# A static schedule for a two-layer mixture-of-experts block: a third group's rows ahead of the last group's, longer gathers in the cost table, constants made at the start

## The chip, the cores and the metric

The kernel runs on one core of a Trainium2 chip. The time is the device time of one launch in microseconds (us): 592.65 us is the median of three runs of the kernel before (590.98 to 595.71). One further execution was recorded by the hardware profiler; it took 534.51 us, and every duration and every point in time below is from that execution, counted from the start of its span.

The engines are named PE (TensorE, matrix products), DVE (VectorE), ACT (ScalarE), POOL (GpSimd) and SP (SyncE, which only issues DMA here). Each runs its own instructions in the order in which they stand in the program, and waits on semaphores for the others.

## The reference

Input are 8 sequences of 256 tokens with 128 features (2048 tokens), float32. Six layers follow each other:

```
x = x + 0.5 * moe(layernorm(x))          # layer 0: 8 experts, top 2 of 8 for every token
x = x + attention(layernorm(x))          # 16 heads of 8, causal
x = x + 0.5 * moe(layernorm(x))          # the same weights again: layer 1
x = x + 0.5 * mix(layernorm(x))          # channel mixing with the token before
x = x + shift(layernorm(x))              # 9 gated shifts (0, +-1, +-4, +-16, +-32), own layernorm
x = x + 0.5 * mix(layernorm(x))

def moe(y):                              # y: rms-normalised rows
    p = top2(softmax(y @ router.T))      # weights of the two experts, summing to 1
    for e in range(8):
        g, u = split(y @ gate_up[e].T)   # 352 hidden features each
        out += p[:, e] * ((silu(g) * u) @ down[e].T)
    return y + clip(alpha) * out

def mix(y):                              # y1: y moved by one token
    r = sigmoid((mu_r*y + (1-mu_r)*y1) @ W_r)
    k = square(relu((mu_k*y + (1-mu_k)*y1) @ W_k))
    return r * (k @ W_v)

def shift(y):
    v = y @ value_W
    out = sum over 9 shifts s of roll(v, -s) * sigmoid(y @ gate_W[s])
    return layernorm(out) * gamma + beta
```

## The kernel before

**Tiling.** The 2048 tokens are 4 groups (`NG`) of 4 x 128 rows (`GT`, `P`). The residual of group g stays on chip as `x[g]` (in the profile x0 to x3 are x_69 to x_72, or plainly x). Dense parts run group by group. In the expert layers each token has two assignments, so 4096 rows are sorted by expert into tiles of 128 rows; with padding these are `TILES` = 39 tiles a layer, every one with one expert.

**An expert layer.** `moe_route` normalises a group, stores its rows to DRAM (`rows0` for the first two groups, `rows1` for all), and finds the top two experts with a product `pl` and DVE's max instructions. `moe_plan` is made twice: once for the first two groups (`whole=False`), which fixes `few` = 9 tiles that these groups fill completely, and once for all groups (`whole=True`), which fixes the other 30. It counts rows per expert, gives every assignment a slot (`end`, `full`, `base`, `until`, `up`, `past`, `slot`), turns the slots into source rows by comparisons (`hit`, `val`, `at`) and small products `pi`, and writes the row lists `take0`, `take1` and the tile's expert. Nearly all of it is DVE work. `moe_experts` then gathers each tile's rows (`xs<-rows,take`, one indirect DMA a tile, issued from POOL), transposes them (`pt`), and `moe_tile` runs the products `pg`, `pu`, the gate `sg`, `hid`, the transposes `ph`, `hT`, the product `po<-dw,hT`, and stores the tile to DRAM by `ys<-ys` from SP. `moe_back` gathers, for each of a group's 4 row blocks and each of the two assignments, the result row by slot (`back<-ys,slot`, 8 indirect DMAs a group, from POOL) and adds it to `x[g]` on DVE.

Slots are ordered so: tiles that groups 0 and 1 fill completely, of which 9 are sure whatever the routing and make the first plan; then one more tile for every expert, which finishes these two groups (tile 24 at the latest); then the rest. So `moe_back` for groups 0 and 1 reads `ys` only up to tile `2*GT*first + E` = 24; groups 2 and 3 read all 39.

**Attention and the last three layers.** `attention` makes two masks, a column of ones `onerow`, and fills the padding of `va` and `mpad` (memsets on POOL); these constants wait for `begun`, an operation of the first layer's weights (`hold["affined"]`). `mix` and `shift` follow per group. In `shift` nine products `pgt` are gated to `p` on DVE; `FOLD` says how many of them POOL adds up (`q`) before PE sums them into one bank with identity products (`po<-ident,q`): (4, 4, 1) means two sums of four and one single, so 3 additions into the bank.

**The order.** `Work` is a list scheduler that runs when the program is built: every operation has an engine, an assumed cost in us, needs, and buffers it takes; the ready operation that can start first goes first, a higher rank (longest path to the end, plus the bias in `BIAS`) wins within 0.3 us. The result is a fixed order on each engine. `BIAS[g]` raises the rank of group g's `moe_back`, `mix` and `shift`; `BIAS[4]` and `BIAS[5]` do so for layer 1's routing and plans. Indirect gathers are entered with 0.98 us on POOL and land 2.7 us (`lag`) later. Where PE would idle in this plan, `keep_warm` puts dummy products `pw<-before,ones_b` in the gap. The recording helper is line 63, which is why all rows name L63.

Of the kernel before, what the change touches and what calls it, by code (L numbers as in the profile page):

```python
# [8 lines left out]
F32 = mybir.dt.float32  # L9
# [10 lines left out]
P = 128  # L20
NG = 4
# [11 lines left out]

BIAS = (25.0, 30.0, 40.0, 55.0, 20.0, 2.0, -6.0)
HC = (0, 128, 224)
ROUND = float(3 * 2**22)
NH = 16
# [7 lines left out]
RMS_EPS = 1e-6  # L47


FOLD = ((4, 4, 1), (4, 4, 1), (4, 4, 1), (4, 2, 1, 1, 1))  # L50


class InOrder:
# [164 lines left out]
def tile_macaron(ctx: ExitStack, tc: tile.TileContext, a: dict, out: bass.AP):  # L218
# [121 lines left out]
    def bank(shape, name):  # L340
        return ps.tile(shape, F32, tag="b", name=name)
# [112 lines left out]
    def moe_layer(n, first):  # L454

        few = 2 * GT * first - 7
        r = {
            "n": n, "first": first, "few": few, "stored": {}, "all_stored": {}, "topped": {},
            "plan": {}, "hold": {},
        }  # L460
        for name, shape, dtype in (
            ("top", [P, NT, 8], F32), ("which", [P, NT, 8], U32), ("w", [P, NT, 2], F32),
            ("ab", [P, 2, NT], F32), ("rs", [P, NT], F32), ("slot", [P, 2 * NT], U32),
            ("take0", [P, few], U32), ("take1", [P, TILES - few], U32), ("expert", [1, TILES], I32),


            ("end", [P, E], F32), ("full", [P, 2, E], F32), ("base", [P, E], F32),
            ("both", [P, E], F32),
        ):
            r[name] = ctile(f"{name}_{n}", shape, dtype)  # L470
        for name, rows in (
            ("rows0", GT * first * P), ("rows1", NT * P), ("ys", TILES * P),
        ):
            r[name] = dram.tile([rows, P], F32, name=f"{name}_{n}", tag=f"{name}_{n}")
        return r
# [126 lines left out]
    def moe_plan(r, whole):  # L602


        few = r["few"]
        nt = NT if whole else GT * r["first"]
        n0, n1 = (few, TILES) if whole else (0, few)
        ns = n1 - n0
# [3 lines left out]
        def small(name, shape, dtype=F32):  # L612

            sizes = dict(zip("abc", shape[1:]))
            wide = 2 * NT * (TILES - 9)
            width = dict(
                oh=2 * NT * E, m=NT * E, slot=NT * E, past=2 * NT * E, sums=P, hit=wide, val=wide,
                le=3 * E, ef=1, eg=1, cb=E, nr=2 * E, at2=2 * E, up=2 * E,
                until=3 * E, whole=E,
            ).get(name, 2 * NT)  # L620
            rows = 1 if shape[0] == 1 else P
            room = wk.tile([rows, width], dtype, tag=name, name=name, bufs=1)
            n = 1
            for m in shape[1:]:
                n *= m
            v[name] = room[0 : shape[0], 0:n]
            if len(sizes) > 1:
                v[name] = v[name].rearrange(
                    f"p ({' '.join(sizes)}) -> p {' '.join(sizes)}", **sizes
                )  # L630
            return v[name]
# [34 lines left out]
        def place():  # L666

            sums = v["sums"]
            pp = bank([P, nt + 1, E], "pp")
            nc.tensor.matmul(  # L670
                pp[:, nt, :], lhsT=sums, rhs=same_e[0 : nt * E], start=True, stop=True
            )
            flat = pp.rearrange("p t e -> p (t e)")[:, 0 : nt * E]
            nc.tensor.matmul(flat, lhsT=before, rhs=v["m"], start=True, stop=False)
            nc.tensor.matmul(
                flat, lhsT=sums, rhs=earlier[0 : nt * E, 0:nt, :].rearrange("p t e -> p (t e)"),
                start=False, stop=True,
            )
            return pp
# [26 lines left out]
        def all_ends():  # L706
            full = r["full"]
            nc.vector.tensor_scalar(full[:, 1, :], full[:, 0, :], float(P), None, ALU.add)
            nc.vector.tensor_tensor(r["both"], r["base"], full[:, 0, :], ALU.add)

            left = small("cb", [P, E])
            nc.vector.tensor_tensor(left, placed.out[:, nt, :], full[:, 0, :], ALU.subtract)
            nc.vector.tensor_scalar(left, left, 63.5, 1.0 / P, ALU.add, ALU.mult)
            nc.vector.tensor_scalar(left, left, ROUND, ROUND, ALU.add, ALU.subtract)
            nr = small("nr", [P, 2, E])
            nc.vector.tensor_scalar(nr[:, 0, :], left, 1.0, None, ALU.min)
            nc.vector.tensor_tensor(nr[:, 1, :], left, nr[:, 0, :], ALU.subtract)

            until = small("until", [P, 3, E])
            nc.vector.tensor_copy(until[:, 0, :], r["end"])  # L720
            for k in range(2):
                nc.vector.tensor_tensor_scan(
                    until[:, k + 1, :], one8, nr[:, k, :], until[:, k, E - 1 : E], ALU.mult, ALU.add
                )


            at2 = small("at2", [P, 2, E])
            nc.vector.tensor_tensor(at2, until[:, 1:3, :], nr, ALU.subtract)
            up = small("up", [P, 2, E])
            nc.vector.scalar_tensor_tensor(  # L730
                up[:, 0, :], at2[:, 0, :], float(P), r["both"], ALU.mult, ALU.subtract
            )
            nc.vector.tensor_tensor(up[:, 1, :], at2[:, 1, :], at2[:, 0, :], ALU.subtract)
            nc.vector.tensor_scalar(up[:, 1, :], up[:, 1, :], -1.0, float(P), ALU.add, ALU.mult)

        def all_slots():
            each, twice = [P, nt, E], [P, nt, 2, E]
            pp, past, slot = placed.out[:, 0:nt, :], small("past", twice), small("slot", each)
            nc.vector.tensor_tensor(
                past, pp.unsqueeze(2).to_broadcast(twice),  # L740
                r["full"].unsqueeze(1).to_broadcast(twice), ALU.is_ge,
            )
            nc.vector.tensor_tensor(past, past, v["up"].unsqueeze(1).to_broadcast(twice), ALU.mult)
            nc.vector.tensor_tensor(slot, pp, r["base"].unsqueeze(1).to_broadcast(each), ALU.add)
            nc.vector.tensor_tensor(past[:, :, 0, :], past[:, :, 0, :], past[:, :, 1, :], ALU.add)
            nc.vector.tensor_tensor(slot, slot, past[:, :, 0, :], ALU.add)

        ended = w.dve(2.4 if whole else 0.9, all_ends if whole else ends, placed, uses=[bp])
        spotted = w.dve(
            1.7 if whole else 0.75, all_slots if whole else slots, ended, uses=[bp]  # L750
        )

        def rows():
# [70 lines left out]
        def which_expert():  # L824


            until = v["until"] if whole else r["end"].unsqueeze(1)
            m = E * (3 if whole else 1)
            le, ef = small("le", [P, m]), small("ef", [P, 1])
            nc.vector.tensor_scalar(  # L830
                le, until.rearrange("p k e -> p (k e)"), float(-n0), tok1[:, 0:1], ALU.add,
                ALU.is_lt,
            )
            nc.vector.tensor_reduce(out=ef, in_=le, axis=AX.X, op=ALU.add)
            if whole:
                eg = small("eg", [P, 1])
                nc.vector.tensor_scalar(eg, ef, -3.5, 1.0 / E, ALU.add, ALU.mult)
                nc.vector.tensor_scalar(eg, eg, ROUND, ROUND, ALU.add, ALU.subtract)
                nc.vector.scalar_tensor_tensor(ef, eg, -float(E), ef, ALU.mult, ALU.add)
# [23 lines left out]
    def moe_experts(r, sizes):  # L863
# [4 lines left out]
        for h in range(2):  # L868
            plan = r["plan"][h]
            rows = r["all_stored" if h else "stored"].values()  # L870
            for n in sizes[h]:
# [14 lines left out]
                got = []  # L886
                for j in range(n):
                    got.append(w.pool(
                        0.98, lambda h=h, k=k0, j=j, f=gather: f(h, k, j), plan["taken"], *rows,
                        **(dict(takes=[xb]) if j == 0 else dict(uses=[xb])), lag=2.7,  # L890
                    ))

# [115 lines left out]
    def moe_back(g, r, stored):  # L1008

        plan, hold = r["plan"][1], r["hold"][g]  # L1010

        until = 2 * GT * r["first"] + E if g < r["first"] else TILES

        def own_rows():
            for t in range(GT):
# [7 lines left out]
        for c in range(2):  # L1023
# [3 lines left out]
            def gather(t, c, box=box):  # L1027
                if t == 0:
# [6 lines left out]

            got = [
                w.pool(
                    0.98, lambda t=t, c=c, f=gather: f(t, c), plan["slots"], *stored[:until],
                    **(dict(takes=[bb]) if t == 0 else dict(uses=[bb])), lag=2.7,
                )  # L1040
                for t in range(GT)
# [15 lines left out]
    BLOCKS = ((0, 0), (1, 0), (1, 1))  # L1057
    LAG = 7

    def attention(begun):  # L1060

# [3 lines left out]
        def constants(mask, step):  # L1067
# [5 lines left out]


        masks = [
            w.pool(1.3, lambda m=m, step=step: constants(m, step), begun)
            for m, step in ((mask_q, -1), (mask_k, 1))
        ]

# [2 lines left out]
            lambda: nc.vector.tensor_reduce(  # L1082
                out=onerow, in_=ident.rearrange("p (j r) -> p j r", r=32)[:, :, DK], axis=AX.X,
                op=ALU.add,
            ), begun,
        )

        va_free = [
            [w.pool(1.4, lambda v=v: nc.gpsimd.memset(v[:, :, :, DK:32], 1.0), begun)] for v in va
        ]  # L1090

        mpad_free = [
            [[w.pool(0.5, lambda m=m: nc.gpsimd.memset(m, 0.0), begun)] for m in row]
            for row in mpad
        ]

# [544 lines left out]
    stored = moe_experts(r0, [[1, 1, 2, *turns(r0["few"] - 4)], turns(TILES - r0["few"])])  # L1641
    for g in range(NG):
        moe_back(g, r0, stored)
    outs = attention(r0["hold"][0]["affined"])
    for g in range(NG):
        changes(g, *outs[2 * g : 2 * g + 2])
        w.back = -BIAS[4] if g < r1["first"] else -BIAS[5]
# [91 lines left out]
```

## Time and profile before

| | us |
|---|---|
| median of three runs (590.98 to 595.71) | 592.65 |
| profiled execution: time | 534.51 |
| its span, first to last instruction | 532.6 |
| PE busy in it | 493.7 (93%) |
| DVE / ACT / POOL busy | 321.5 / 254.2 / 229.7 |
| dummy products pw, 119 of them | 33.6 |
| xs gathers, 78 on POOL: busy, mean | 75.1, 0.962 |
| back gathers, 64 on POOL: busy, mean | 61.4, 0.959 |

The stages, by the timeline: loads, routing and plans of layer 0 to 33 us; its expert tiles from 33 to some 160 us, with attention entered at 122; attention to 302; layer 1's tiles from 300 to 427; mix, shift and mix from 404 to 528; the last store after that. Mean granted TensorE clock is 0.971 of full speed.

A row of the timeline gives start, duration, engine, line, operation, output<-inputs, shapes and count, and in brackets how long the engine stood idle before it and whose event ended the idle time. A busy PE includes the dummy products, which compute nothing that is used; idle time is therefore read as gaps plus `pw` rows.

### The profile page before, as it was taken

The page shows a single profiled execution, that of the slowest core. Times are in us where ns is not written, and L with a number is a line of the kernel's source. Part 1 is how long each engine was busy: PE and PEld are TensorE (multiplying, and loading weights), DVE is VectorE, ACT ScalarE, POOL GpSimd, SP SyncE. Part 2 cuts the span into 40 slices and gives each one's busy share as a digit, 9 for nine tenths or more (in the row PEclk, how much of TensorE's full clock was granted, in tenths as well). Part 3 has the DMA queues.
Part 4 walks back from the last instruction along what each step waited for, and adds up shares of the span by engine and source line. Part 5 has one row for each costly group of instructions (what it writes and reads, how often), then busy time and mean ns, then how long its engine had stood idle before and what let it go on. Part 6 is the DMA issues. An engine that isn't in the chain of part 4 may idle for free.

```text
span 532.6 us, 12554 instructions
## 1 busy us (share of the span) xinstructions
PE 493.7 (93%) x4619; PEld 350.4 (66%) x4619; DVE 321.5 (60%) x1139; ACT 254.2 (48%) x536; POOL 229.7 (43%) x239
## 2 busy tenths in 40 slices
PE   7969989889999999999999999979998996999985
PEld 3537767676776767777777775758775842667564
DVE  7768333455857886777774577333353333878981
ACT  3223455535155446456545641465445572464743
POOL 5150789675005600000002502795373368677641
PEclk9779999999999999999999998999998999899998
DMA  8830222232001100000100110313431011000001
GB/s 282 294 95 26 75 59 59 54 72 51 14 16 46 48 2 3 2 22 3 61 4 11 36 51 18 92 46 72 55 79 31 12 49 45 0 1 1 2 23 57
DMA packets 27035, 26.24 MB, mean 49 GB/s; under 512 B 4064, under 2 KB 24288, under 8 KB 26560
## 3 DMA queue, kind: packets, MB, share of 16 engines
q1 hardware_dynamic: 21232, 15.60, 9.2%
q0 software_dynamic: 4544, 9.32, 8.0%
q8 instruction: 38, 0.62, 0.5%
q10 hardware_dynamic: 1200, 0.53, 0.4%
q14 instruction: 21, 0.17, 0.1%
HBM read 17.18 MB, written 9.31 MB: 50 GB/s over the span
## 4 chain that ended last, share of the span: by engine, by line
PE 58%; POOL 15%; DVE 10%; issue 7%; DMA 6%; ACT 3%; POOLq 0%; SPq 0%; ACTq 0%; DVEq 0%
PE sc L63 15%; PE po L63 11%; PE pg L63 7%; PE pu L63 6%; POOL back L63 6%; PE pt L63 4%; PE ph L63 4%; POOL q L63 2%; PE pr L63 2%; DMA rows<-n 2%; POOL xs L63 2%; DVE stats L63 2%; DMA rest<-in_rest 2%; PE pw L63 2%; PE pk L63 2%
## 5 line engine op out<-in xcount | busy, mean ns | idle before, releaser
L63 POOL DMA_INDIRECT xs<-rows,take x78 | 75.1, 962 | 120.2 <-DVE take L63 41.8
L63 POOL DMA_INDIRECT back<-ys,slot x64 | 61.4, 959 | 59.7 <-DMA ys<-ys 34.3
L63 ACT ACTIVATE ep<-sc 128x512 f32<-128x512 f32 x96 | 52.0, 595 | 55.7 <-PE sc L63 55.7
L63 PEld LDWEIGHTS po<-dw,hT 128*128 128x128 f32 x468 | 62.8, 192 | 21.2 <-ACT hT L63 5.5
L63 PE MATMUL po<-dw,hT 128*128 x468 | 65.9, 279 | 5.3 <-ACT hT L63 3.8
L63 DVE TENSOR_TENSOR hid<-sg,pu 128x352 f32<-128x352 f32 x78 | 40.3, 519 | 48.8 <-PE pu L63 34.6
L63 POOL TENSOR_TENSOR stats<-stats,minus_half 128x4 f32<-128x4 f32 x28 | 28.6, 1023 | 87.7 <-DVE stats L63 87.3
L63 ACT COPY hT<-ph 128x384 f32<-128x384 f32 x78 | 37.1, 477 | 58.1 <-PE ph L63 54.7
L63 PE MATMUL pg<-gu,nT 128*128 x156 | 61.6, 477 | 0.5 <-ACT nT L63 0.5
L63 PE MATMUL pu<-gu,nT 128*128 x156 | 60.5, 470 | 0.0
L63 PEld LDWEIGHTS sc<-kT,qT 32*128 32x128 f32 x768 | 45.8, 186 | 19.2 <-issue 16.4
L63 ACT ACTIVATE sg<-pg 128x352 f32<-128x352 f32 x78 | 36.0, 463 | 41.0 <-PE pg L63 38.3
L63 PE MATMUL sc<-qT,kT 32*128 32x128 f32 x768 | 55.5, 283 | 0.0
L63 PE MATMUL sc<-kT,qT 32*128 32x128 f32 x768 | 54.6, 283 | 0.9 <-DVE mpad L63 0.9
L63 DVE TENSOR_REDUCE mtmp<-sc 128x4 f32<-128x512 f32 x64 | 41.5, 685 | 20.3 <-PE sc L63 20.0
L63 PEld LDWEIGHTS sc<-qT,kT 32*128 32x128 f32 x768 | 46.5, 186 | 2.1 <-issue 2.1
L63 PE MATMUL ph<-ident,hid 128*128 128x128 f32 x234 | 39.1, 279 | 4.4 <-DVE hid L63 4.4
L63 PEld LDWEIGHTS ph<-ident,hid 128*128 128x128 f32 x234 | 29.2, 144 | 17.9 <-DVE hid L63 6.9
L63 PE MATMUL pw<-before,ones_b 128*128 128x512 bf16 x119 | 33.6, 433 | 7.0 <-DVE p L63 4.5
L63 DVE COPY ys<-po 128x128 f32<-128x128 f32 x78 | 21.9, 288 | 21.6 <-PE po L63 17.0
L63 PE MATMUL pgt<-yTg,rest 128*128 128x512 f32 x72 | 33.4, 597 | 0.3 <-ACT yTg L63 0.2
L63 PEld LDWEIGHTS pu<-gu,nT 128*128 128x128 f32 x156 | 26.7, 196 | 7.3 <-issue 0.9
(197 smaller groups left out, 880.9 us busy)
## 6 DMA issues: line engine op xcount, KB each, us to landing
ys<-ys SPq DMA_DIRECT2D x78, 64.0 KB, 1.6
gu<-in_guT SPq DMA_DIRECT2D x2, 1408.0 KB, 8.1
rest<-in_rest SPq DMA_DIRECT2D x1, 1280.0 KB, 8.4
xs<-rows,take POOLq DMA_INDIRECT x78, 2.6
x<-in_x SPq DMA_DIRECT2D x4, 256.0 KB, 4.4
dw<-in_dwT SPq DMA_DIRECT2D x1, 1024.0 KB
rows<-rows SPq DMA_DIRECT2D x2, 512.0 KB
back<-ys,slot POOLq DMA_INDIRECT x64, 2.6
```

The source lines that it names most:

```text
L63: ins = do(*args, **kw)
```

## The change

Five edits:

1. In layer 1, the whole plan gets a third part (`soon` = 3): after the tiles that finish groups 0 and 1 come tiles that group 2's rows fill further, ahead of those that need the last group's. One more product counts the rows of groups 0 to 2, and DVE gets more small instructions and one wider comparison and product (`past` has 3 parts in place of 2). `moe_back` of group 2 then reads `ys` only up to tile `2*GT*3 + E` = 32.
2. Gathers are entered in the schedule with 1.25 us in place of 0.98.
3. Attention's constants no longer wait for `begun`.
4. `BIAS` has new values: the groups' are 10, 28, 18, 0 in place of 25, 30, 40, 55; routing and plan of layer 1's last two groups get 22 in place of 2, those of its first two 19 in place of 20.
5. Group 1's shift is folded as (2, 2, 2, 2, 1) in place of (4, 4, 1).

```diff
-BIAS = (25.0, 30.0, 40.0, 55.0, 20.0, 2.0, -6.0)
+BIAS = (10.0, 28.0, 18.0, 0.0, 19.0, 22.0, -6.0)
-FOLD = ((4, 4, 1), (4, 4, 1), (4, 4, 1), (4, 2, 1, 1, 1))
+FOLD = ((4, 4, 1), (2, 2, 2, 2, 1), (4, 4, 1), (4, 2, 1, 1, 1))
...
+        soon = first + 1 if n == 1 and first + 1 < NG else None
...
-            ("end", [P, E], F32), ("full", [P, 2, E], F32), ("base", [P, E], F32),
+            ("end", [P, E], F32), ("full", [P, 3, E], F32), ("base", [P, E], F32),
...
     def moe_plan(r, whole):
-        few = r["few"]
+        few, soon = r["few"], r["soon"] if whole else None
+        parts = 3 if soon else 2
...
         def place():
+            if soon:
+                rows = slice(0, GT * soon * E)
+                nc.tensor.matmul(
+                    pp[:, nt + 1, :], lhsT=sums[rows, :], rhs=same_e[rows], start=True, stop=True
+                )
...
         def all_ends():
-            nc.vector.tensor_scalar(nr[:, 0, :], left, 1.0, None, ALU.min)
-            nc.vector.tensor_tensor(nr[:, 1, :], left, nr[:, 0, :], ALU.subtract)
+            nc.vector.tensor_scalar(nr[:, 0, :], left[:, 0, :], 1.0, None, ALU.min)
+            if soon:
+                nc.vector.tensor_tensor(nr[:, 2, :], left[:, 0, :], nr[:, 0, :], ALU.subtract)
+                nc.vector.tensor_scalar(nr[:, 1, :], left[:, 1, :], -1.0, 0.0, ALU.add, ALU.max)
+                nc.vector.tensor_tensor(nr[:, 2, :], nr[:, 2, :], nr[:, 1, :], ALU.subtract)
+                nc.vector.scalar_tensor_tensor(
+                    full[:, 2, :], nr[:, 1, :], float(P), full[:, 1, :], ALU.mult, ALU.add
+                )
+            else:
+                nc.vector.tensor_tensor(nr[:, 1, :], left[:, 0, :], nr[:, 0, :], ALU.subtract)
...
-            for k in range(2):
+            for k in range(parts):
                 nc.vector.tensor_tensor_scan(
...
+            if soon:
+                nc.vector.tensor_tensor(up[:, 2, :], up[:, 2, :], nr[:, 1, :], ALU.subtract)
+                nc.vector.tensor_scalar(up[:, 2, :], up[:, 2, :], float(P), None, ALU.mult)
         def all_slots():
-            each, twice = [P, nt, E], [P, nt, 2, E]
+            each, twice = [P, nt, E], [P, nt, parts, E]
...
-            nc.vector.tensor_tensor(past[:, :, 0, :], past[:, :, 0, :], past[:, :, 1, :], ALU.add)
-            nc.vector.tensor_tensor(slot, slot, past[:, :, 0, :], ALU.add)
+            for k in range(parts):
+                nc.vector.tensor_tensor(slot, slot, past[:, :, k, :], ALU.add)
...
-                        0.98, lambda h=h, k=k0, j=j, f=gather: f(h, k, j), plan["taken"], *rows,
+                        1.25, lambda h=h, k=k0, j=j, f=gather: f(h, k, j), plan["taken"], *rows,
...
     def moe_back(g, r, stored):
-        until = 2 * GT * r["first"] + E if g < r["first"] else TILES
+        until = TILES
+        if g < r["first"]:
+            until = 2 * GT * r["first"] + E
+        elif r["soon"] and g < r["soon"]:
+            until = 2 * GT * r["soon"] + E
...
-                    0.98, lambda t=t, c=c, f=gather: f(t, c), plan["slots"], *stored[:until],
+                    1.25, lambda t=t, c=c, f=gather: f(t, c), plan["slots"], *stored[:until],
...
-    def attention(begun):
+    def attention():
-            w.pool(1.3, lambda m=m, step=step: constants(m, step), begun)
+            w.pool(1.3, lambda m=m, step=step: constants(m, step))
...
-            [w.pool(1.4, lambda v=v: nc.gpsimd.memset(v[:, :, :, DK:32], 1.0), begun)] for v in va
+            [w.pool(1.4, lambda v=v: nc.gpsimd.memset(v[:, :, :, DK:32], 1.0))] for v in va
...
-            [[w.pool(0.5, lambda m=m: nc.gpsimd.memset(m, 0.0), begun)] for m in row]
+            [[w.pool(0.5, lambda m=m: nc.gpsimd.memset(m, 0.0))] for m in row]
```

**What it does to the order** (read from the two programs' instruction lists; no time is in them). POOL: the masks and memsets stand ahead of the first gather of layer 0, two of the `mpad` fills and one of `va` between the second and third power instruction of routing. In layer 1, the 16 back gathers of groups 0 and 1 (group 1's first) are followed directly by group 2's eight, and group 3's eight come after group 1's `x += rv`; the last two of them stand behind group 2's `x += rv`. Group 3's first gather waits on seven store semaphores again. PE: before, the mix products of groups 0 and 1 stand among the last layer-1 tiles; in the changed kernel only group 1's do, at the same tile (36 `pg` done), and after the last tile come the mix products of groups 0 and 2, then group 1's shift. Dummies: 24 become 33 at the whole plan of layer 1; after the last tile 3 + 28 + 3 become 3 + 3 + 4, and at the end 3 + 3 + 2 become 3 + 13 + 3. The groups are stored in the order 1, 2, 0, 3 in place of 3, 1, 0, 2.

## The prediction

> **What bounds the kernel now.** I read the page's slices first. PE is the busiest row, at 9 tenths almost everywhere from the tenth slice on, so the end is set by PE's work plus the stretches where PE does nothing useful.
>
> ```profile
> PE   7969989889999999999999999979998996999985
> ...
> PEclk9779999999999999999999998999998999899998
> ```
>
> The 35th slice (440 to 453 us) is the lowest after the start. The windows by stage show it (columns: stretch, its length, busy us and count of PE, PEld, DVE, ACT, POOL, then granted clock, DMA share, GB/s), and the same windows for the dummy products alone show how much of "busy" is empty (PE busy, clock, DMA).
>
> ```profile
> 318.00:328.00 10.00, 9.51 (x59) 5.01 (x57) 9.48 (x43) 0.00 (x0) 0.00 (x0) 1.00 0.01 2
> ...
> 427.00:441.00 14.00, 13.54 (x37) 5.92 (x35) 5.15 (x20) 10.50 (x24) 9.95 (x11) 1.00 0.18 47
> 441.00:455.00 14.00, 8.71 (x35) 3.80 (x35) 6.63 (x24) 2.52 (x7) 11.76 (x12) 0.85 0.16 39
> 455.00:509.00 54.00, 53.64 (x273) 36.80 (x272) 46.78 (x144) 31.10 (x67) 37.68 (x33) 0.98 0.00 1
> ```
>
> ```profile
> 318.00:328.00 10.00, 5.18 (x24) 1.00 0.01 2
> ...
> 441.00:455.00 14.00, 7.40 (x31) 0.85 0.16 39
> ```
>
> So there are two holes: 318 to 328, where DVE is full (9.48 of 10), and 441 to 455, where POOL is (11.76 of 14). The timeline of PE, then of POOL, explains the second:
>
> ```profile
> 435.26 5.31 PE L63 MATMUL pgt<-yTg,rest 128*128 128x512 f32 x12
> 441.59 6.20 PE L63 MATMUL pw<-before,ones_b 128*128 128x512 bf16 x28 [1.02 <-DVE p L63]
> 448.80 1.48 PE L63 MATMUL pt<-ident,y 128*128 128x128 f32 x4 [1.01 <-ACT y L63]
> 453.81 1.44 PE L63 MATMUL pw<-before,ones_b 128*128 128x512 bf16 x3 [3.52 <-DVE p L63]
> 455.04 0.64 PE L63 MATMUL pr<-wrp,yTs 128*128 128x128 f32 x2
> ```
>
> ```profile
> 429.76 1.02 POOL L63 DMA_INDIRECT back<-ys,slot  x1 [0.34 <-issue]
> ...
> 450.79 0.95 POOL L63 DMA_INDIRECT back<-ys,slot  x1 [0.30 <-issue]
> 451.75 2.50 POOL L63 TENSOR_TENSOR q<-p 128x512 f32<-128x512 f32 x2
> ```
>
> The last tile's store leaves at 427.1; 2.7 us later groups 2 and 3 begin 16 gathers, one each 1.25 us (0.94 busy, 0.30 between), and POOL is not free for sums until 451.75. Groups 0 and 1 feed PE until 440.6, then nothing is ready. The first hole ends here; POOL stood idle 23.42 us for the plan:
>
> ```profile
> 328.12 1.02 POOL L63 DMA_INDIRECT xs<-rows,take  x1 [23.42 <-DVE le L63]
> ```
>
> **What the Trainium skill says.** "TensorE: Matmul & The Clock Gate", Part 1, says that an idle window of about 3.4 us halves PE's clock. The trace agrees: behind the hole pairs of `pr` products come every 0.43 us, later in the same run every 0.22. "SBUF — State Buffer", Who interferes with whom, says that a DVE instruction with two SBUF inputs and a GpSimd instruction that reads SBUF exclude each other. The trace agrees in kind: `x<-back,w,x` takes 0.342 us in the median and up to 1.36. "Perfetto Trace Analysis", DMA Instruction — SWDGE, says the reported end of such a DMA is the end of descriptor writing, not of the transfer; a back gather lands 2.5 us after issue in the median.
>
> **The change part by part**, against the profiled execution's 534.5 us.
>
> (1) *Constants early.* Between the gathers of layer 0 (78.0 to 96.9 us) the masks and memsets stretch six intervals to 2.01, 1.70, 1.67, 2.98, 3.78 and 2.59 us; six plain ones are 7.5, one `rs` power in between costs 1.59, so 14.73 - 7.5 - 1.59 = 5.6 us leave POOL's row. PE's own gaps between 56 and 136 us sum to 6.8; those whose cause is POOL or a gather (1.99 and 0.56 via DVE's wait for `rs`, 0.58 via `w`, 1.92 for xs) to 5.1. Value: -1.5, ends 0 and -5. What the early place costs: 0.54 + 0.54 + 1.39 = 2.5 us ahead of the third power, of which 0.94 was idle. I cost it at nothing: rows go out and weights come in by DMA until 33.45, where `pg` starts. Without that cover it would be 1.5.
>
> (2) *Longer whole plan.* Six more small DVE instructions of about 0.17 us, spaced about 0.2: 1.2. Two `past` instructions grow from 256 to 384 elements (0.28 at 128, 0.42 at 256, so about 0.56): 0.3. One more addition: 0.3. Sum 1.8, all on the path, since the first hole is DVE's; queued behind on DVE are the `hid` of three tiles, and behind these PE. The extra count product (0.17) is hidden beside it. Ends +1.2 and +3. `pi` of the first plan stands one score batch (2 us) later on PE; the same hole absorbs it as long as six tiles still fit in front (they took 302 to 317.8). Ends 0 and +2.
>
> (3) *One mix fewer among the tiles.* The mix of one group is pt 0.44, pk 1.72, pr 1.78, pv 0.9 = 4.85 us on PE and moves behind the last tile: the last tile ends earlier and later work grows by as much, net 0. The gap at 402.2 (2.0 us for `y`, whose power stood behind all 16 gathers until 402.37) goes: the power now stands behind 13. Value -2, ends -2.5 and 0. Last tile: 427.0 + 1.8 - 4.85 - 2.0 = 421.9.
>
> (4) *Group 2's gathers early.* Back gathers began at 382.4 (store of tile 24 landed at 381.4); now 384.2. Sixteen of them and one power (1.3 with its gap) end at 405.5. Tile 32's store: the 34th `po` is due around 403 with landing. So group 2's eight run 405.5 to 415.5, land by 418, and its `y` reaches PE near 423.5, while group 0's mix runs. Group 3's begin when the last store lands, 421.9 + 2.7 = 424.6, and end near 436; PE needs its rows only near 453. The hole is gone: 14.0 less 0.6 of transposes is 13.4, 1.5 of slow clock behind it, 1.1 of four stray dummies up to 509: -16. In return PE has no shift work at hand when tiles end: three entries (pt, ACT copy 0.6, pk) leave it waiting about 1.2 to 2 us each: +5, ends +3 and +9. Net -11.
>
> (5) *Fold.* Two more sums into the bank, 4 products in 0.9 each: +1.8 on PE. Two POOL additions fewer (2.5) lie off the path.
>
> (6) *Order at the end.* From the last sum (508.9) to PE's last product took 17.7 us, a chain over DVE, POOL, ACT; beside it stood 10.6 us of other groups' products, now 9.7, so 0.9 moves in front: +0.9. Last store (SP, one DMA) unchanged.
>
> The gather's cost alone moves places, not work; it is in (3) and (4). Sum: -1.5 + 1.8 - 2 - 11 + 1.8 + 0.9 = -10.0: 534.5 becomes 524.5, or 0.981.
>
> **To the median.** The runs take 592.65, 10.9% above the profiled execution, and no row says where. If PE is what is slower, groups 0 and 1 last 1.5 us longer into the hole, and less is won: I take 1.6% rather than 1.9%: 583.
>
> **Rivals.** *R1, nothing that counts:* PE now has no spare work behind the last tile, and entries cost 12 in place of 5. -10 + 7 = -3: 589. For it: DVE and ACT waited 3.5 to 7 us for such chains at 402 and 448. Against: groups 0 and 2 arrive spaced. *R2, slower:* POOL's row. Eleven gathers stand behind group 1's power, which waits for DVE; or group 2's gathers wait for all stores after all (the change not doing what it says). Then its `y` comes at 424.6 + 10 + 2.6 + 3.7 = 441, PE stands from 427 to 441, the 5 becomes 17 to 21: +2 to +6, so 537 to 541, at the median 595 to 600. It decides from about 10 us late (433). Against: group 3's first gather waits anew on seven store semaphores, 39 - 32. *R3, more:* the first layer gives 5 and entries 3: -15.5, 575.
>
> **Chances.** Forecast 0.46, R3 0.17, R1 0.25, R2 0.12. Within 1% (586.7 to 598.6) is about what a measurement can't tell from no change. R1 and a rim of R2 lie there, a little of the forecast too: faster 0.64, same 0.26, slower 0.10. The range, 572 to 597, reaches from R3's far side over R1 to R2's near end.
>
> **What would show it.** PE: fewer than 5 dummies in a row and no gap over 3 us between the last tile and the last sum. POOL: group 2's gathers before the last store. The hole at the whole plan 1.8 longer. Gathers in layer 0 at 1.25 apart. It is wrong if PE waits behind the last tile for over 10 us, or the hole grows over 4.

## The result

| | median us | runs |
|---|---|---|
| before | 591.82 | 4, 586.61 to 595.71 |
| after | 584.58 | 4, 581.67 to 585.74 |

The ratio is 0.9887, with a 95% interval of 0.9841 to 0.9934: 7.2 us less, against 583 us forecast. One thing has to be known to read what follows: the timed runs of one comparison, before and after alike, fall together into one of two conditions, a quick one in which the kernel before takes some 535 us and a long one in which it takes 583 to 594, and the profiled execution of before shown ahead of the prediction was of the quick kind, while the timed runs above and the profile of after are of the long kind. So I set beside each other only timed runs of one comparison, and stages of profiles of one condition. In the quick condition the change later gave 0.961 (0.957 to 0.965).

### The profile page after: what moved, and what is told of

Same layout as the page of the kernel before. It is cut to its first block, busy times and chain, and to the rows that moved or that the text cites. A ratio compares the mean times of both kernels' runs of the same rounds, so it can differ in the third digit from the quotient of the medians.

```text
span 582.3 us, 12609 instructions
## 1 busy us (share of the span) xinstructions
PE 517.5 (89%) x4642; PEld 363.5 (62%) x4642; DVE 324.2 (56%) x1146; ACT 254.3 (44%) x536; POOL 226.9 (39%) x237
## 4 chain that ended last, share of the span: by engine, by line
PE 67%; DVE 11%; issue 7%; another core or an unknown queue 5%; DMA 4%; ACT 3%; POOL 2%; POOLq 0%; SPq 0%; DVEq 0%; ACTq 0%
PE po L63 15%; PE sc L63 15%; PE pg L63 8%; PE pu L63 8%; PE ph L63 5%; PE pt L63 4%; DVE x L63 2%; PE pgt L63 2%; PE pr L63 2%; DMA rows<-n 2%; DVE p L63 1%; PE pm L63 1%; PE pv L63 1%; DMA rest<-in_rest 1%
## 5 line engine op out<-in xcount | busy, mean ns | idle before, releaser
L63 PEld LDWEIGHTS po<-dw,hT 128*128 128x128 f32 x468 | 67.2, 207 | 41.7 <-issue 18.9
L63 PE MATMUL po<-dw,hT 128*128 x468 | 72.2, 295 | 23.2 <-issue 12.1
L63 PE MATMUL pg<-gu,nT 128*128 x156 | 64.3, 496 | 3.4 <-issue 1.8
L63 PE MATMUL pu<-gu,nT 128*128 x156 | 62.6, 484 | 0.0
L63 DVE COPY ys<-po 128x128 f32<-128x128 f32 x78 | 22.4, 291 | 46.4 <-PE po L63 20.1
L63 PE MATMUL ph<-ident,hid 128*128 128x128 f32 x234 | 41.9, 291 | 5.2 <-issue 4.7
L63 PEld LDWEIGHTS ph<-ident,hid 128*128 128x128 f32 x234 | 31.0, 151 | 22.2 <-issue 16.2
L63 PE MATMUL po<-ep,va 128*32 128x128 f32 x768 | 30.2, 288 | 5.2 <-issue 5.2
```

The lines of the kernel that those rows point to most:

```text
L63: ins = do(*args, **kw)
```

## The profile after

The profiled execution of after took 584.18 us (span 582.3). Its slices, PE's busy tenths and its granted clock:

```profile
PE   7969489987997889999999799879897799999995
...
PEclk9779699998998789999999899779898799999998
```

There is no low slice behind the last tile any more: slices 33 to 39, 466 to 568 us, are all 9. The lower digits stand in the expert tiles (slices 5 and 10, 26 and 27, 31 and 32) and at the start of attention (13 to 15), where before had mostly 9s. Such standstills belong to the long condition: run 12, further down, shows them in the kernel before too.

Four windows of after (the ten us ahead of the whole plan's first gather; 14 us up to the last tile's copy at 482.95; 14 us behind it; 54 us from there), and under them the dummy products alone:

```profile
358.00:368.00 10.00, 9.73 (x55) 5.09 (x53) 9.69 (x45) 0.00 (x0) 0.00 (x0) 0.95 0.00 0
469.00:483.00 14.00, 13.97 (x90) 10.90 (x89) 9.24 (x46) 6.42 (x16) 7.12 (x7) 1.00 0.16 44
483.00:497.00 14.00, 14.00 (x71) 9.06 (x70) 2.97 (x16) 10.74 (x25) 9.53 (x10) 1.00 0.13 36
497.00:551.00 54.00, 51.92 (x242) 32.15 (x241) 49.13 (x139) 34.24 (x78) 39.85 (x35) 1.00 0.03 8
```

```profile
358.00:368.00 10.00, 4.95 (x23) 0.95 0.00 0
469.00:483.00 14.00, 1.62 (x6) 1.00 0.16 44
483.00:497.00 14.00, 1.03 (x4) 1.00 0.13 36
```

The 14 us behind the last tile hold 14.00 us of PE, of which 1.03 are dummies, at full clock. Before, the hole was in the second 14 us behind the last tile (441 to 455), so the fair measure is the 28 us from that tile on. In these PE spent 14.0 us on products that are used in the kernel before (22.25 busy, 8.21 of it dummies) and 25.7 us in the kernel after (26.70 and 1.03). The kernel before has the same hole in the long condition, with 14.2 us of used products (22.26 and 8.07); this is its longest row in run 12:

```profile
505.20 6.20 PE L63 MATMUL pw<-before,ones_b 128*128 128x512 bf16 x28 [1.02 <-DVE p L63]
```

The hole ahead of the whole plan has stayed: 4.95 us of dummies in ten. POOL shows why the first closed, and what the second costs:

```profile
368.79 1.02 POOL L63 DMA_INDIRECT xs<-rows,take  x1 [25.33 <-DVE take L63]
```

```profile
463.19 0.95 POOL L63 DMA_INDIRECT back<-ys,slot  x1 [4.78 <-DVE x L63]
...
473.01 0.95 POOL L63 DMA_INDIRECT back<-ys,slot  x1 [0.30 <-issue]
...
485.83 1.02 POOL L63 DMA_INDIRECT back<-ys,slot  x1 [1.78 <-issue]
...
496.46 1.05 POOL L63 DMA_INDIRECT back<-ys,slot  x1 [0.30 <-issue]
```

POOL waits 25.33 us for the whole plan, 1.9 more than before (run 12 has 23.51 in the long condition). Group 2's eight gathers run from 463.19, twenty us ahead of the last tile's copy, and group 3's begin 2.9 us behind it. On PE no more than four dummies stand in a row there:

```profile
479.49 0.81 PE L63 MATMUL pw<-before,ones_b 128*128 128x512 bf16 x3
...
480.57 0.81 PE L63 MATMUL pw<-before,ones_b 128*128 128x512 bf16 x3
...
485.45 1.03 PE L63 MATMUL pw<-before,ones_b 128*128 128x512 bf16 x4
...
500.60 1.32 PE L63 MATMUL pt<-ident,y 128*128 128x128 f32 x4 [0.44 <-DVE p L63]
```

The entries of the groups into their mix (`pt` to `pk`), which I had priced at 5 us, take 2.65 us of dummies, and PE's first idle time behind them is the 0.44 us at 500.60. The pairs of `pr` behind them come every 0.22 us where they came every 0.43 behind the hole.

## The experiments

All ratios are to the kernel before of the same comparison. The four comparisons were of runs 1 to 4 (before 534.9 us), 5 to 8 (583.4), 9 to 11 (534.2) and 12 (594.1). Below, "the tail" is what lies between the copy of layer 1's last tile and the end, "the front" what the change does ahead of that, in layer 0 above all.

| run | what it is | median us | ratio (95%) |
|---|---|---|---|
| 1 | before | 535.8 | 1.001 (0.998 to 1.004) |
| 2 | after, group 2 waits for all stores | 524.9 | 0.983 (0.980 to 0.986) |
| 3 | after, no third part | 523.8 | 0.981 (0.977 to 0.985) |
| 4 | before, constants early | 534.0 | 0.996 (0.993 to 0.999) |
| 5 | after | 577.5 | 0.989 (0.983 to 0.994) |
| 6 | before, constants early, cost 1.25 | 592.2 | 1.013 (1.008 to 1.018) |
| 7 | as 6, new BIAS | 588.6 | 1.010 (1.007 to 1.013) |
| 8 | after, old BIAS | 603.9 | 1.036 (1.030 to 1.041) |
| 9 | after | 513.0 | 0.961 (0.957 to 0.965) |
| 10 | as 2 | 525.4 | 0.985 (0.980 to 0.989) |
| 11 | after, old fold | 516.1 | 0.967 (0.963 to 0.971) |
| 12 | before | 591.3 | 0.998 (0.995 to 1.002) |

### Runs 1 and 12: the kernel before in both conditions

No edit.

> The kernel before, unchanged, for a second profiled execution. Its first one took 534.5 us where its timed runs took 587 to 596, the one of the kernel after 584.2. If that first execution was an odd one, this one takes 585 to 596 us, and the extra 50 us lie in its two stretches of expert tiles, not in attention. If the profile itself makes this kernel quick, it takes 530 to 540 again. Ratio to itself 1.000, within 0.004. In both cases the hole behind the last tile is there: more than 25 dummy products (pw) within 20 us of the last tile, and the last tile's copy lies 104 to 108 us ahead of the end.

> The kernel before once more, for a profiled execution of it in the condition of the recorded comparison, in which it takes 580 to 596 us rather than 535. If it falls there: theory that the lost time is the same three stretches as in the kernel after (ACT or DVE standing for over 3 us for a releaser that the profile doesn't know, beside a run of gathers on POOL, at the first tiles after the whole plan, at the second part of layer 0 and at attention's first back gathers), 45 to 58 us more than the quick execution, and a tail from the last tile to the end of 105 to 112 us. Rival: the slower clock or slower DMAs spread the loss evenly, attention too. If it takes 530 to 540 us, it tells neither, and where the recorded pair lost part of its gain stays open.

Run 1 was quick again (profiled span 535.2), run 12 was not (595.9; that execution took 598.18 us, some 7 above the median of its runs, so differences of a few us from it don't count). Run 12 is later than run 1 by 13.5 us at the copy of layer 0's last tile, by 27.2 more from there to the last write of layer 1's first plan (`expert`), by 0.6 to that of its whole plan, by 20.1 in layer 1's tiles, and by -0.6 from the last tile to the end. So the loss is not spread evenly: two stretches have none of it. Of the 60.7 us, 37 are idle time of PE (77.3 against 40.2) and 24 are longer busy time (518.5 against 494.8); the products are longer in the stages that have the standstills, where the granted clock is lower too (attention 0.917 against 1.000, layer 1's tiles 0.912 against 0.976), and not in the tail. The standstills lie at gathers. These are ACT's waits of run 12, at the first tiles behind both whole plans:

```profile
66.31 0.48 ACT L63 COPY hT<-ph 128x384 f32<-128x384 f32 x1 [6.03 <-remote]
```

```profile
385.48 0.48 ACT L63 COPY hT<-ph 128x384 f32<-128x384 f32 x1 [9.10 <-remote]
```

"remote" is a releaser that the profile does not know. The same DVE instruction of the kernel after shows it best, in run 9 (quick) and then in run 5 (long):

```profile
158.27 0.69 DVE L63 TENSOR_REDUCE mtmp<-sc 128x4 f32<-128x512 f32 x1 [1.27 <-PE sc L63]
```

```profile
186.64 0.69 DVE L63 TENSOR_REDUCE mtmp<-sc 128x4 f32<-128x512 f32 x1 [10.10 <-remote]
```

In both, POOL is issuing the eight back gathers of one group, from 155.60 and from 175.24. In run 9 DVE follows PE after 1.27 us; in run 5 it stands for 10.10. All six profiles of the long condition have such a wait before an `mtmp` within 16 us behind layer 0's last tile, 5.3 to 10.2 us; in the eight of the quick one no `mtmp` waits longer than 2.3. I expected run 12 to lose 45 to 58 us, in stretches, with a tail of 105 to 112: the medians differ by 56, and its tail is 105.5, as in the quick condition (105.9 and 106.1).

### Runs 2, 3, 5, 9 and 10: group 2's gathers

Runs 5 and 9 are the kernel after, unchanged:

> The kernel after, unchanged, beside a kernel before that takes some 535 us rather than 590. In the run in which group 2 waits for all stores (525 us) 15.2 us of dummy products stand behind the last tile; in the kernel after 2.7 us. If the early gathers close that hole, this one is 9 to 13 us below that run: 512 to 517 us, ratio 0.957 to 0.967. Rival: the early gathers only move the wait (POOL, or entries without spare work), 522 to 526 us, ratio 0.976 to 0.984.

> The kernel after, unchanged, on the same chip as the next two. The chips differ: the kernel before takes 535 us on one and 583 on another, so only runs of one chip are set beside each other. Where before takes some 535 us, I expect 512 to 518, ratio 0.957 to 0.969 (the run that waits for all stores had 0.983 there, with 15.2 us of dummies where this kernel has 2.7). Where before takes 580 or more, 0.984 to 0.994 as in the two comparisons so far. Rival: the early gathers don't matter, and the ratio is that of the next run.

Run 5 met the long condition, and gave the recorded ratio again, 0.989. What run 9's expectation says of the chips is wrong: runs 5 to 8 and 9 to 11 ran on the same one, and met different conditions. Runs 2 and 10 are the kernel after with

```diff
         until = 2 * GT * r["first"] + E
-    elif r["soon"] and g < r["soon"]:
-        until = 2 * GT * r["soon"] + E
```

> The kernel after, but the back gathers of group 2 wait for the stores of all 39 tiles again, as those of groups 0, 1 and 3 beyond the first part do; the third part of the plan stays. Theory of the tail (the gain is the closed hole, net -11 us): the hole comes back, group 2's y reaches PE some 18 us later, ratio to the kernel before 1.003 to 1.012. Rival of the front (the gain is the constants' and the gathers' new places): 0.988 to 0.993, as the kernel after.

> The kernel after with group 2's gathers waiting for all stores, beside the kernel after on the same chip. Theory of the tail: 9 to 13 us more than the kernel after, on any chip, that is 1.7 to 2.3% (ratio 0.980 to 0.986 on the quick chip, 1.005 to 1.015 on the slow one), with 35 or more dummies within 30 us of the last tile. Rival: equal to the kernel after within 0.4%.

Run 2 fell below both ranges that I had given it and seemed to speak for the front: 0.983, while after had only 0.989. That was two conditions set beside each other. In one comparison, run 9 has 512.97 us and run 10 525.35: the early gathers are worth 12.4 us, within the 9 to 13 expected. PE's timeline behind the last tile, run 10 and then run 9:

```profile
424.22 8.37 PE L63 MATMUL pw<-before,ones_b 128*128 128x512 bf16 x38
...
441.58 1.89 PE L63 MATMUL pw<-before,ones_b 128*128 128x512 bf16 x8
...
446.53 1.24 PE L63 MATMUL pw<-before,ones_b 128*128 128x512 bf16 x5
```

```profile
407.30 0.81 PE L63 MATMUL pw<-before,ones_b 128*128 128x512 bf16 x3
...
408.38 0.81 PE L63 MATMUL pw<-before,ones_b 128*128 128x512 bf16 x3
...
413.26 1.03 PE L63 MATMUL pw<-before,ones_b 128*128 128x512 bf16 x4
```

Run 10's first line alone is 38 dummies, 8.37 us, up to the next group's `pt`; all in all it has 65 of them between 409 and 452, run 9 has 10 in its whole transition. The hole comes back where the wait does. What run 2 keeps against before all the same, some 10 us, is mostly not the tail: by the profiles of runs 2 and 1 (9.0 us apart), 6.9 are won by the last tile of layer 0 and 3.4 behind the last sum. The first of these I had priced at 1.5.

Run 3 leaves the third part out as well:

```diff
-    soon = first + 1 if n == 1 and first + 1 < NG else None
+    soon = None
```

> The kernel after without the third part: the whole plan has two parts again, and group 2 waits for all stores. Against the run that only waits, the plan's DVE instructions are back at the old length: 1.8 us less, ratio 0.997 lower than that run's if the plan is on the path; equal to it if the plan is hidden. Theory of the tail: 1.000 to 1.009 against the kernel before. Rival of the front: 0.985 to 0.991.

Its ratio, 0.981, lies below both ranges too. It takes 1.0 us less than run 2, inside the intervals of both. Its profile is sharper: POOL's wait for the whole plan is 24.05 us, against 25.64 in run 10 and 25.54 in run 9, so the longer plan costs 1.5 to 1.6 us on the path, where I had put 1.8.

### Run 4: constants early

The third edit of the change, in the kernel before.

```diff
-    def attention(begun):
+    def attention():
...
-            w.pool(1.3, lambda m=m, step=step: constants(m, step), begun)
+            w.pool(1.3, lambda m=m, step=step: constants(m, step))
...
-            [w.pool(1.4, lambda v=v: nc.gpsimd.memset(v[:, :, :, DK:32], 1.0), begun)] for v in va
+            [w.pool(1.4, lambda v=v: nc.gpsimd.memset(v[:, :, :, DK:32], 1.0))] for v in va
```

> The kernel before, with attention's constants made first and nothing else changed; the order of PE, DVE and ACT hardly moves. Theory of the tail: POOL's row gets 5.6 us shorter among layer 0's gathers, of which PE sees 1.5 us (0 to 5): ratio 0.997 (0.991 to 1.000). Rival of the front: most of the gain is here, 0.988 to 0.991.

0.996, as expected: some 2 us (0.9 by the medians). The first xs gather left at 25.32 us, 1.4 later than before (23.88): the loads that I had named as cover for the third power did not cover it, and the 1.5 us that I gave for that case were paid. More than that was won back among the tiles: against run 1, of the same comparison, the last tile of layer 0 is copied 2.2 us earlier (160.1 against 162.3). The first profile of before has it at 159.8, so two executions of one kernel differ by that much.

### Runs 6, 7 and 8: the gather's cost and BIAS

Run 6 is run 4 with the new cost in both gathers:

```diff
-                        0.98, lambda h=h, k=k0, j=j, f=gather: f(h, k, j), plan["taken"], *rows,
+                        1.25, lambda h=h, k=k0, j=j, f=gather: f(h, k, j), plan["taken"], *rows,
```

Run 7 adds the new BIAS; run 8 is the kernel after with the old one:

```diff
-BIAS = (10.0, 28.0, 18.0, 0.0, 19.0, 22.0, -6.0)
+BIAS = (25.0, 30.0, 40.0, 55.0, 20.0, 2.0, -6.0)
```

> The kernel before with two parts of the change: constants early and the gather's cost of 1.25 in the schedule. No third part, old BIAS, old fold. If the gather's cost is what reorders the work well, most of the 11 us that the run without a third part shows (524 us) are here: 523 to 527, ratio 0.978 to 0.986. If BIAS does it: 532 to 537, ratio 0.995 to 1.005, with the hole behind the last tile (more than 25 dummies) still there. My prediction gave the cost alone nothing.

> The run before this one with the new BIAS added; it is the kernel after without the third part and with the old fold of group 1. If BIAS does it: 522 to 525, ratio 0.976 to 0.982, groups 0 and 1 later among the tiles and the last tile near 407 us rather than 427. The new fold should cost 1.8 us of PE, so this run is 0 to 2 us below the run that has the fold but no third part (523.8). Rival: the fold matters, and this one stays at 528 or more.

> The kernel after with the old BIAS. If the early gathers alone close the hole, as my prediction had it, 513 to 520 us, ratio 0.960 to 0.973, near the kernel after. If the order of the work under the new BIAS is what closes it (spare work of groups 0 and 1 held back behind the last tile), 526 to 534, ratio 0.985 to 0.999.

The comparison fell into the long condition, for which these numbers were not made, and none of the three ratios lies in a range that I gave for a theory; so only the differences count. Constants and cost, with or without BIAS, lose 1.0 to 1.3% here, and BIAS alone moves little (588.6 against 592.2). Run 7 and the kernel after (run 5) differ by the third part and the fold alone, and these are worth 11.1 us (588.6 against 577.5), more than the whole change gains in this comparison. With the third part the same BIAS is worth 26 us (603.9 against 577.5): neither theory had room for that. In run 8 group 2's gathers do run early (the last one at 478, the last tile's copy at 485.8), but 116.1 us lie between that copy and the end, against 99.4 in run 5. Its PE line:

```profile
485.57 2.32 PE L63 MATMUL pw<-before,ones_b 128*128 128x512 bf16 x10
...
499.48 3.83 PE L63 MATMUL pw<-before,ones_b 128*128 128x512 bf16 x17
...
574.10 5.34 PE L63 MATMUL pw<-before,ones_b 128*128 128x512 bf16 x24
```

All four groups' first mixes stand behind the last tile here, against three in run 5: 4.9 us more. Two groups come at once (`pt` at 487.7 and 489.0) and the next two find nothing beside them: 39 dummies from 485 to 520 us, 9.40 us, against 10 and 2.65. At the end 39 stand again, 9.23 us, against 19 and 4.59. The three differences make 16.2 of the 16.7; another 8.4 us of run 8's loss lie ahead of the whole plan's last write, where the old BIAS ranks routing and plan lower. Early rows were worth something here only with the groups spaced so that each fills the other's entry.

### Run 11: the fold

```diff
-FOLD = ((4, 4, 1), (2, 2, 2, 2, 1), (4, 4, 1), (4, 2, 1, 1, 1))
+FOLD = ((4, 4, 1), (4, 4, 1), (4, 4, 1), (4, 2, 1, 1, 1))
```

> The kernel after with group 1's fold as it was, two sums on POOL in place of two on PE. My sum says 1.8 us less on PE: ratio 0.003 below the kernel after. Rival: with group 1 now the last or last but one to be summed, POOL's additions (1.25 us each, two more) stand on its chain to the end, and this one is 1 to 6 us slower than the kernel after (ratio 0.002 to 0.011 above it).

The rival was right in size: 516.06 against 512.97, the old fold costs 3.1 us. Its reason, POOL's chain, is not what the profile shows; on PE it is this first row, at the last tile:

```profile
408.18 4.91 PE L63 MATMUL pw<-before,ones_b 128*128 128x512 bf16 x22
...
413.37 1.03 PE L63 MATMUL pw<-before,ones_b 128*128 128x512 bf16 x4
```

That is 26 dummies where run 9 has 10, 3.3 us more. I had counted the products that the new fold adds (1.8 us) and called two POOL additions "off the path"; in the order planned with the new fold these 16 dummies are gone. Why the plan comes out so was not followed up.

## Why the prediction was right, and where its sum was not

The forecast of 583 was met (584.58), and the central step held. The sum of -10.0, made against the quick profiled execution, did not: between that execution (532.6) and run 9 (509.4) it is -23.2 (-21.2 by the medians of run 9's comparison), of which idle time of PE makes 18.2 (38.9 against 20.7). In the table a plan ends with its last write, `expert`, and a tile with its copy.

| stage, ended by | predicted | measured | in it |
|---|---|---|---|
| last tile of layer 0 | -1.5 | -7.7 | step 1, the gather's cost |
| layer 1's first plan | 0 | +0.4 | |
| whole plan | +1.8 | -2.2 | step 2 |
| last tile | -6.9 | -6.7 | step 3 |
| last sum | -4.4 | -3.8 | steps 3 (the mix that moves), 4, 5 |
| end | +0.9 | -3.4 | step 6 |

- **Step 4, the closed hole: right.** Counted from the first back gather of layer 1, I had group 2's at 21.3 us, the last tile at 37.7 and group 3's at 40.4; run 9 has 22.2, 38.2 and 41.1. Dummies and gaps at the last tile and up to the first sums fall from 14.0 (8.45 and 5.56) to 3.4 (2.65 and 0.75). The early gathers taken away alone cost 12.4, against a net 11.
- **Step 3: right in size, in part by luck.** The tile stage is shorter by what was foretold, 6.7 us. PE's idle time in it falls from 6.1 to 0.6; of this the gap of 2.0 at 402 was in my sum, but another of 2.9 at 351, where `po` waited for `hT`, was not, and in return the stage holds one tile more than before.
- **Step 2: right.** 1.5 to 1.6 us measured (runs 9 and 10 against run 3) within 1.2 to 3. The stage is shorter all the same, by 2.2 us to its last write; to its first gather it is 0.8 longer. In before the gathers start 3 us ahead of that last write, in run 9 together with it. I did not foresee this.
- **Step 1: right in size** (2 us), wrong on what covers the third power.
- **The sentence that failed: "The gather's cost alone moves places, not work".** Up to layer 0's last tile, run 9's order is that of run 6 (constants and cost alone), instruction by instruction, but for one addition of the plan that the third part rewrites; so there it differs from run 4's through that cost alone. The last tile is copied at 160.1 us in run 4 (159.8 and 162.3 in the two quick profiles of before), at 152.2 in run 9, and at 152.6 to 155.4 in runs 2, 3, 10 and 11, which have the same order of layer 0: 4.7 to 7.9 us for the cost. PE's gaps from 45 us to that tile, over 0.15 us each, sum to 7.8 us in before, 7.0 in run 4 and 3.1 in run 9. The waits of PE in that window show which ones went, before and then run 9 (columns: instruction, what it waited for, us, times, longest):

```profile
PE ph L63 <- DVE hid L63: 3.6, 4, 2.0
PE pt L63 <- DMA xs<-rows,take: 1.9, 1, 1.9
PE po L63 <- ACT hT L63: 0.9, 2, 0.5
```

```profile
PE pg L63 <- issue: 2.0, 1, 2.0
PE pt L63 <- PE po L63: 0.8, 1, 0.8
PE po L63 <- ACT hT L63: 0.3, 1, 0.3
```

  The waits on `hid` and on a gather that landed late are gone. That the order puts tiles where their rows are, now that the table has a gather's true interval of 1.25 us, is my reading of this. The gaps are 4.7 of the 7.7 us; the rest is shorter busy time of PE, which I have not placed. The cost was not run without the other parts in the quick condition, and in the long one run 6 was slower than before.
- **Steps 5 and 6: wrong in sign.** The fold gains 3.1 where I had a loss of 1.8. The end is 3.4 shorter, not 0.9 longer: from the last sum to PE's last product it is 14.4 us (489.05 to 503.40), against 17.7. The new order leaves two groups' final mixes behind the last sum (`pk` at 490.2 and 498.7) where before had three (508.8, 516.3 and 522.0). The third did not vanish: used products behind the last sum take 9.7 us against 14.7, so 5 us moved in front of it, where I had 0.9, and stand in the row above, which is shorter all the same.
- **The scaling to the median: the right number for a wrong reason.** I took 1.6% in place of 1.9% for what a slower PE would leave of the hole. What happened is that the condition of the recorded pair leaves the tail untouched (105.5 us in run 12, 99.4 in both profiles of after: -6.2, where the pair's medians have -7.2) and takes most of the rest. Little of the front's gain is seen there: PE's gaps of over 0.8 us from 45 to 150 us are 12.3 in run 12 and 15.7 and 14.8 in the two profiles of after, and the last tile of layer 0 comes 0.2 and 4.0 us earlier in these. A sum too small by 11 to 13 us (medians, profiles) met a condition that took away 14 to 16: that the forecast of 583 was hit is luck, though the closed hole is not. The kernel that waits for all stores was not run in that condition; what the early gathers are worth there rests on the profiles' tails and on runs 5 and 7.
- **Slips of reading, without weight in the sum:** the low slice of before is the 34th, not the 35th; a back gather lands 2.6 us after issue in the median, not 2.5; `x<-back,w,x` has a median of 0.344 us, not 0.342.

Of the rivals, R3 (entries 3 us, first layer 5) came nearest to the quick condition: 2.65 and 7.7. R1's entries of 12 and R2's late `y` did not come; run 8 shows that a slower outcome was near all the same, by an order of mixes that I had not priced: **BIAS has no line of its own in the sum**, though with the third part it decides 26 us (run 8 against run 5).

Open stay what the "remote" waits are, and which part loses the front's gain in that condition: run 6 is slower than before there by 1.3%, but against run 12's profile no stage of it stands out, and the two are of different comparisons, whose kernels before are 11 us apart.

## What to carry to other kernels

When a static order is planned from a cost table, price the table's entries as a change of their own: here a more nearly true interval of one instruction was worth 4.7 to 7.9 us in one stage of the quick condition, and was given nothing. A hole behind a barrier closes when something is allowed to start ahead of it, but here only an order that leaves work for each entry turned that into time; try the two together and each without the other. And before a sum made on a profile is carried over to timed runs, see that the profiled execution takes their time: 534 against 592 us here was a warning that part of the sum might not be seen.

## What the runs showed of the hardware

The same program takes 513 or 577 us (after) and 534 to 536 or 583 to 594 us (before), by comparison. The second and third comparison, which differ so, ran on one chip, the first and fourth on another. The excess is not spread: PE and ACT, and often DVE, stand for 3 to 10 us while POOL issues indirect gathers, and at the same stages of both kernels (run 12 has PE gaps of 4.1, 3.0, 3.3 and 7.0 us at 63, 133, 182 and 379 us; run 5 of 4.4, 1.6, 5.9 and 2.4 at 60, 130, 181 and 378). Stretches with gathers but without it exist too, such as the one behind the last tile, so gathers alone don't explain it. The idle time makes 37 of the 60.7 us between runs 1 and 12; the other 24 are longer products in the same stages, at a lower granted clock. Whether the lower clock follows from the standstills or goes with their cause is not shown. No run was made to find the cause.
